# Moving the attention-times-values matmuls of layer 2's rounds to the end of the round

## The chip, the cores and the metric

The kernel runs on one core of a Trainium2 chip. The metric is the device time of one execution in microseconds (us); of several runs the median is given. The engines named below are PE (matrix multiplication, with its weight loads as PEld), DVE (vector), ACT (scalar, activation functions), POOL (a third elementwise engine) and SP (which issues the DMAs here). Each engine runs its instructions strictly in its own order and waits for others by semaphores, so an instruction that waits holds up everything queued behind it.

## The reference

The program computes a transformer of four layers on a batch of B = 4 sequences of S = 512 tokens with D = 128 channels. The change touches layer 2's second attention, a mixture of experts over the value and output projections, with H = 16 heads of P = 64 and E = 8 experts:

```python
def _moe_attn(x, Wq, Wk, Wv, Wo, Wsel_v, Wsel_o):
    q = _rope(jnp.einsum('bsd,hdp->bhsp', x, Wq))
    k = _rope(jnp.einsum('bsd,hdp->bhsp', x, Wk))
    gv = _gate(x, Wsel_v)
    v = jnp.einsum('bsd,bhse,hedp->bhsp', x, gv, Wv)
    att = jax.nn.softmax(jnp.einsum('bhsp,bhtp->bhst', q, k) / np.sqrt(P), axis=-1)
    o = jnp.einsum('bhst,bhtp->bhsp', att, v)
    go = _gate(x, Wsel_o)
    return jnp.einsum('bhsp,bhse,hepd->bsd', o, go, Wo)
```

`_gate` gives each token, for each head, a weight for each of the eight experts (zero for all but two). `_rope` turns the first 32 channels of q and k by the token's position. Everything here is fp32.

## The kernel before, in words

**Rounds.** Layer 2's attention is done in 32 passes, each one sequence and one pair of heads. `l2_ffn` (L1719 on) turns them into 32 rounds and a short 33rd. Round t holds the attention of pass t (`attend`), the output projection of pass t-1 (`finish`), and the projections of pass t+1 (`project`).

`attend(t)` is the round's main list. `score(0, 1)` and `score(2, 3)` (L1811) make for two of the four blocks of 128 queries, and for both heads, a 128 x 512 block of scores (the matmuls `mm<-roped`), and `exps` (L1905) takes each block's maxima on DVE (L1911, written `at_m`) and its exponentials on ACT (L1913, `at_e`), whose sums are kept aside. `turn(i)` (L1820) transposes block i with eight small matmuls (L1825), and ACT copies the result into `eT` (L1826). `invert` (L1828) takes the reciprocals of the sums, transposes them on DVE and sends them to DRAM (`inverted`, L1834). `spread_sums` (L1838) asks for the first part of the output gates `c` (`spread(0)`, the DMAs of L1807) and then brings the reciprocals back over all partitions as `d` (L1843). `values` (L1845) asks for the second part of `c`, multiplies the transposed exponentials by the values in 8 matmuls (L1850) and lets DVE multiply the result by `d` in place (`mm<-mm,d`, the multiplication by d).

`finish(t)` has nine steps `expert(0)` to `expert(8)`: expert e multiplies that result by the gate of expert e on DVE (`og<-mm,c`), and the matmul of expert e-1 (L1878) adds into one PSUM bank. The last step adds the bank into `y`. `project(t)` has ten steps: `rope` (two matmuls, two ACT operations `qk`, two DVE operations `roped`, four DMAs `rot`), eight `value` steps (a matmul `mm<-w_l_ffn_qkv,xT` or the like, and a multiplication by the input gates on DVE, `gvx<-mm,gv`; POOL adds up the experts) and `rope_rest`, two DVE operations.

**The order within a round.** The nineteen steps of `finish` and `project` are merged evenly into one list, the fill:

    rope e0 v0 e1 v1 e2 v2 e3 v3 e4 rope_rest e5 v4 e6 v5 e7 v6 e8 v7

`emit` (L1921) places the fill between the main steps by weights. After each main step it issues fill steps until the share of the fill that is issued equals the share of the weights that is passed:

```python
passed += w
until = len(fill) * passed // total
```

Three rounds are different: in round 16 the fill is not merged (first all of `finish`, then a weight load, then all of `project`), in round 31 it is `finish` alone, and the short 33rd is nothing but `finish`.

**The side chains.** Beside the rounds other work is issued in small steps, by `weave`: a step of the chain for every 3.3 steps of the rounds in rounds 0 to 14 (layer 2's other attentions and gates for sequences 2 and 3), for every 4.5 in rounds 15 to 24 and for every 2.6 in the rest (the dense layers of the finished sequences, layer 3's projections). `dense` is `l2_dense` (L1934). Their usual pieces are statistics of a normalisation on DVE (L470 to L490, ending in `nmr` or `nr_b`), four ACT operations that apply them (L492, `xn` or `d_z`), transposes on PE (L516, L1944) and their copy on ACT (L517), and additions such as `x<-x,...`.

**What sets the order on the engines.** The code is written for a tile framework with a list scheduler: the order in which the steps are issued gives each instruction its priority, and the scheduler then sets each engine's order by that priority and its own estimate of when operands are ready. So a change in the order of the steps moves instructions on every engine, also those of the side chains. PSUM has eight banks, seven of them (`mm`) shared in turn by scores, projections, transposes, the value result and the bank of `finish`; the eighth (`s`) belongs to the side chains. The buffers of `c` are four, those of `eT` two, of `og` three.

Of the kernel before, what the change touches and what calls it, by code (L numbers as in the profile page):

```python
# [291 lines left out]
class Net:  # L292
# [1428 lines left out]
    def l2_ffn(self, pool, gv, y, away, passes, feed, wants, late):  # L1721
# [70 lines left out]
        def attend(t):  # L1792


            b, hp = passes[t]
            m = made[t]
            den = sums[t % 2]
            eT = [pool.tile([P, TB, S], F32, tag=f"eT{hl}", name="eT") for hl in range(2)]
            es = {}

            def spread(part):

                c = m["c", part] = pool.tile([P, 2, S], F32, tag="c", name="c", bufs=4)
                for hl in range(2):
                    at = (2 * hp + hl) * E + 2 * part
                    src = away[b, at : at + 2].rearrange("e s -> (e s)")
                    nc.sync.dma_start(  # L1807
                        c[64 * hl : 64 * hl + 64].rearrange("p e s -> p (e s)"), src.partition_broadcast(64)
                    )

            m["spread"] = spread  # L1811

            def score(*at):
                for i in at:
                    ss = [self.mm() for _ in range(2)]
                    for hl in range(2):
                        r = slice(64 * hl, 64 * hl + 64)
                        self.dot(ss[hl], (m["q"][r, i * P : i * P + P], m["k"][r, :]))
                    es[i] = [self.exps(ss[hl], den[:, TB * hl + i : TB * hl + i + 1], pool, 6) for hl in range(2)]

            def turn(i):
                for hl in range(2):
                    p = self.mm((P, TB, P))
                    for j in range(TB):
                        nc.tensor.transpose(p[:, j, :], es[i][hl][:, j * P : j * P + P], self.ident)  # L1825
                    nc.scalar.copy(eT[hl][:, :, i * P : i * P + P], p)  # L1826

            def invert():  # L1828

                nc.vector.reciprocal(den[:, : 2 * TB], den[:, : 2 * TB])  # L1830
                turned = pool.tile([P, 32], F32, tag="turned", name="turned")
                nc.vector.transpose(turned, den)
                for k in range(4):
                    nc.sync.dma_start(  # L1834
                        inverted[t % 2][:, :, k, :].rearrange("h j r -> (h j) r"), turned[32 * k : 32 * k + 2 * TB, :]
                    )

            def spread_sums():  # L1838
                spread(0)
                m["d"] = pool.tile([P, S], F32, tag="d", name="d")  # L1840
                for hl in range(2):
                    src = inverted[t % 2][hl].rearrange("j k r -> (j k r)")
                    nc.sync.dma_start(m["d"][64 * hl : 64 * hl + 64, :], src.partition_broadcast(64))  # L1843

            def values():  # L1845
                spread(1)
                po = self.mm()
                for j in range(TB):
                    for hl in range(2):
                        nc.tensor.matmul(  # L1850
                            po[64 * hl : 64 * hl + 64, :], lhsT=m["v"][:, j, hl, :], rhs=eT[hl][:, j, :],
                            start=j == 0, stop=j == TB - 1,
                        )
                self.tt(po, po, m.pop("d"), ALU.mult)
                m["o"] = po

            return [
                (lambda: score(0, 1), 4), (lambda: turn(0), 1), (lambda: score(2, 3), 1), (lambda: turn(1), 2),
                (invert, 0), (lambda: turn(2), 2), (lambda: turn(3), 2), (spread_sums, 1), (values, 4),
            ]  # L1860

        def finish(t):
# [26 lines left out]
        def rounds(first, last):  # L1889
            if first == 0:  # L1890
                for step in project(0):
                    step()
                    yield
            for t in range(first, last):
                if t in wants:
                    self.want(wants[t])
                done, new = finish(t - 1), project(min(t + 1, n))
                if t in late:
                    fill = done + [lambda: self.want(late[t])] + new
                else:  # L1900
                    fill = self.merged(done, new)
                yield from self.emit(attend(t) if t < n else [(lambda: None, 1)], fill)
# [606 lines left out]
```

## Time and profile before

| what | us |
|---|---|
| median of 5 runs | 2229.02 |
| lowest and highest run | 2227.91, 2236.06 |
| the profiled execution | 2238.19 |
| its span, first to last instruction | 2236.5 |
| the rounds of layer 2 in it | 925 to 1910 |
| a round, first scores to the next first scores: shortest and longest of the 31 that begin and end in scores | 23.27 (round 0), 37.68 (round 25) |
| a round with no side chain work (15, 24, 30) | 26.96 |

The profiled execution is one run, 9.2 us above the median; differences within it are read from it, and absolute times are compared by medians. In the profile a row of the timeline gives the start, the duration (of a group of like instructions, then with their number behind x), the engine, the source line, the operation with output and input names, and in brackets the idle time that the engine had before it and the instruction that ended the wait. An fp32 matmul shows as two passes, so that "x2" is one matmul over 512 columns; the next group starts while the last pass is still draining, so the pitch from start to start is what PE needs (0.43 a pass), and a group's duration is a little longer.

### The profile page before, as it was taken

The numbers are of one execution on the slowest core, as the hardware profiler recorded it, in microseconds if no ns is written. First come the engines' busy times: TensorE is split into PE (matmuls) and PEld (weight loads), VectorE is DVE, ScalarE is ACT, GpSimd is POOL, SyncE is SP. The second block draws the span as 40 slices with busy tenths as digits, with TensorE's granted clock in tenths as the row PEclk, the third lists the DMA queues.
The fourth block names the chain that finished last, engine by engine and source line by source line (L and its number), as shares of the span: only waits on it lengthen the run. The fifth ranks groups of instructions, "written<-read, shape, count | busy, mean of one in ns | idle before, by whom it ended". The sixth has DMA issues, their size and how long they took to land.

```text
span 2236.5 us, 28168 instructions
## 1 busy us (share of the span) xinstructions
PE 2106.9 (94%) x8982; PEld 1116.6 (50%) x8988; DVE 1604.0 (72%) x4045; ACT 1003.1 (45%) x2040; POOL 568.7 (25%) x705
## 2 busy tenths in 40 slices
PE   6999899999999999899999999999999999699887
PEld 3556556645544554444444444444444444466543
DVE  7676566477675768787977788777866787588735
ACT  4555544543433554344444443434433454156532
POOL 1000000000000000433332334333333354135733
PEclk8898899999999999999999999999999999899978
DMA  6321144254445343334343345445444445321122
GB/s 169 94 72 45 27 122 113 68 127 108 112 103 141 76 122 87 84 87 110 103 120 97 102 120 123 122 108 136 119 132 123 103 124 133 70 96 34 31 73 78
DMA packets 92115, 224.37 MB, mean 100 GB/s; under 512 B 22226, under 2 KB 41106, under 8 KB 91710
## 3 DMA queue, kind: packets, MB, share of 16 engines
q1 hardware_dynamic: 88398, 218.63, 37.0%
q0 software_dynamic: 3568, 3.93, 0.7%
q8 instruction: 71, 1.16, 0.2%
q14 instruction: 78, 0.64, 0.1%
HBM read 193.43 MB, written 23.53 MB: 97 GB/s over the span
## 4 chain that ended last, share of the span: by engine, by line
PE 73%; DVE 17%; ACT 4%; issue 3%; POOL 1%; DMA 1%; another core or an unknown queue 1%; SPq 0%; DVEq 0%; ACTq 0%; POOLq 0%
PE mm L426 19%; PE f L426 13%; PE s L426 8%; PE mm L1878 8%; PE acc L1037 6%; PE mm L1850 5%; PE mm L1825 4%; DVE h L437 2%; PE mm L1205 1%; PE mm L1160 1%; PE mm L1227 1%; DVE m L1167 1%; DVE at_m L1911 1%; DVE x L437 1%; PE acc L2274 1%
## 5 line engine op out<-in xcount | busy, mean ns | idle before, releaser
L1786 POOL TENSOR_TENSOR gvx<-gvx 128x512 f32<-128x512 f32 (+1 forms) x256 | 263.4, 1029 | 537.3 <-DVE gvx L437 459.4
L426 PE MATMUL f<-xT,w_l_ffn 128*128 128x512 f32 (+1 forms) x700 | 338.3, 605 | 1.2 <-ACT h L1029 0.7
L1913 ACT ACTIVATE at_e<-mm,at_m 128x512 f32<-128x512 f32 x256 | 172.9, 685 | 263.6 <-DVE at_m L1911 258.3
L426 PE MATMUL mm<-w_l_ffn_qkv,xT 128*128 128x512 f32 x512 | 265.3, 604 | 4.1 <-ACT at_e L1913 2.0
L1878 PE MATMUL mm<-og,w_l_ffn_o 128*128 128x512 f32 x512 | 263.3, 600 | 3.2 <-DVE og L437 1.9
L437 DVE TENSOR_TENSOR h<-h,f 128x512 f32<-128x512 f32 (+1 forms) x192 | 131.4, 686 | 152.5 <-PE f L426 109.4
L1029 ACT ACTIVATE h<-f 128x512 f32<-128x512 f32 x189 | 112.4, 596 | 246.9 <-PE f L426 209.2
L1037 PE MATMUL acc<-h,w_l_ffn 128*128 128x512 f32 x378 | 198.6, 610 | 3.6 <-DVE h L437 2.9
L426 PEld LDWEIGHTS f<-xT,w_l_ffn 128*128 128x128 f32 (+1 forms) x700 | 126.7, 191 | 133.1 <-issue 112.8
L437 DVE TENSOR_TENSOR gvx<-mm,gv 128x512 f32<-128x512 f32 x256 | 174.3, 684 | 25.7 <-PE mm L426 21.5
L437 DVE TENSOR_TENSOR og<-mm,c 128x512 f32<-128x512 f32 x256 | 173.8, 683 | 22.1 <-PE mm L1878 20.3
L1911 DVE TENSOR_REDUCE at_m<-mm 128x1 f32<-128x512 f32 x256 | 161.5, 683 | 13.0 <-PE mm L426 12.4
L1826 ACT COPY eT<-mm 128x512 f32<-128x512 f32 x256 | 137.3, 595 | 70.1 <-PE mm L1825 69.7
L1825 PEld LDWEIGHTS mm<-ident,at_e 128*128 128x128 f32 x1024 | 119.5, 141 | 66.9 <-issue 46.1
L1878 PEld LDWEIGHTS mm<-og,w_l_ffn_o 128*128 128x128 f32 x512 | 91.1, 190 | 114.9 <-issue 87.6
L1825 PE MATMUL mm<-ident,at_e 128*128 128x128 f32 x1024 | 134.8, 274 | 3.6 <-ACT at_e L1913 3.6
L426 PEld LDWEIGHTS mm<-w_l_ffn_qkv,xT 128*128 128x128 f32 x512 | 87.2, 191 | 92.8 <-issue 54.7
L426 PE MATMUL mm<-roped 64*128 64x512 f32 x512 | 131.2, 623 | 1.6 <-DVE roped L437 1.3
L1167 DVE TENSOR_REDUCE m<-mm 128x1 f32<-128x512 f32 (+3 forms) x176 | 105.5, 637 | 35.5 <-PE mm L1163 34.6
L1850 PE MATMUL mm<-eT,v 128*64 128x512 f32 x512 | 120.8, 606 | 2.1 <-ACT eT L1826 2.1
L1037 PEld LDWEIGHTS acc<-h,w_l_ffn 128*128 128x128 f32 x378 | 72.1, 195 | 89.0 <-issue 62.7
L437 DVE TENSOR_TENSOR h<-h,c 128x512 f32<-128x512 f32 x160 | 110.6, 697 | 3.9 <-DMA c<-l_ffn_w 1.1
(496 smaller groups left out, 3575.8 us busy)
## 6 DMA issues: line engine op xcount, KB each, us to landing
c<-gates SPq DMA_DIRECT2D x256, 256.0 KB
c<-l_ffn_w SPq DMA_DIRECT2D x96, 384.0 KB
w_l_ffn_qkv<-in_l_ffn_qkv SPq DMA_DIRECT2D x24, 640.0 KB
w_l_ffn<-in_l_ffn SPq DMA_DIRECT2D x26, 576.0 KB
w_l_ffn_o<-in_l_ffn_o SPq DMA_DIRECT2D x24, 512.0 KB
rot<-qk SPq DMA_DIRECT2D x128, 64.0 KB
d<-inverted SPq DMA_DIRECT2D x64, 128.0 KB
k_parts<-k SPq DMA_DIRECT2D x12, 384.0 KB
```

Of the source, the lines that this page charges most:

```text
L426: self.nc.tensor.matmul(out, lhsT=lhsT, rhs=rhs, start=i == 0, stop=i == len(pairs) - 1)
L437: self.nc.vector.tensor_tensor(out, a, b, op)
L1029: nc.scalar.activation(h, pg, AF.Silu)
L1037: nc.tensor.matmul(acc["t"], lhsT=W["d" + u], rhs=h, start=i == 0, stop=i == n - 1)
L1167: nc.vector.tensor_reduce(m[:, i, h0 : h0 + per], ps, AX.X, ALU.max, negate=True)
L1786: nc.gpsimd.tensor_tensor(x[:, :, :m], x[:, :, :m], x[:, :, m : 2 * m], ALU.add)
L1825: nc.tensor.transpose(p[:, j, :], es[i][hl][:, j * P : j * P + P], self.ident)
L1826: nc.scalar.copy(eT[hl][:, :, i * P : i * P + P], p)
L1850: nc.tensor.matmul(po[64 * hl : 64 * hl + 64, :], lhsT=m["v"][:, j, hl, :], rhs=eT[hl][:, j, :], start=j == 0, stop=j == TB - 1,)
L1878: nc.tensor.matmul(acc, lhsT=W["o"][:, (e - 1) * D : e * D], rhs=hs.pop(e - 1), start=e == 1, stop=e == E)
L1911: nc.vector.tensor_reduce(m, s, AX.X, ALU.max, negate=True)
L1913: nc.scalar.activation(e[:, :n], s, AF.Exp, bias=m, accum_out=den)
```

## The change

The weights of the last three main steps are changed. `turn(3)` weighs 3 in place of 2, `spread_sums` 4 in place of 1, and `values` 0 in place of 4. The sum of the weights stays 17.

```diff
-                (invert, 0), (lambda: turn(2), 2), (lambda: turn(3), 2), (spread_sums, 1), (values, 4),
+                (invert, 0), (lambda: turn(2), 2), (lambda: turn(3), 3), (spread_sums, 4), (values, 0),
```

With the fill of 19 the order of steps at a round's end becomes, where it was `turn(3), e5, v4, spread_sums, e6, values, v5, e7, v6, e8, v7` and then the next round's `score(0, 1)`: `turn(3), e5, v4, e6, spread_sums, v5, e7, v6, e8, v7, values` and then `score(0, 1)`. In round 31, whose fill is the nine steps of `finish` alone, e6, e7 and e8 stood behind the values and stand ahead of them, and the first steps of `finish(31)` follow the values directly. Nothing is added to or taken from the work.

## The prediction

> **What bounds the kernel now.** I read four views in this order: the page's first lines, the busy time of each engine over the stretch of layer 2's rounds, the waits of PE and DVE in that stretch, and then the timeline of one undisturbed round and of the few rounds with a stall.
>
> The page's head and, below it, the stretch from 925 to 1910 us, which holds all 32 rounds (columns: span of the window, its length, busy time and instruction count of PE, PEld, DVE, ACT, POOL, granted clock, DMA share, GB/s):
>
> ```profile
> span 2236.5 us, 28168 instructions
> PE 2106.9 (94%) x8982; PEld 1116.6 (50%) x8988; DVE 1604.0 (72%) x4045; ACT 1003.1 (45%) x2040; POOL 568.7 (25%) x705
> ...
> 925.00:1910.00 985.00, 962.51 (x3616) 455.33 (x3616) 763.96 (x1479) 428.36 (x990) 363.76 (x436) 0.99 0.44 115
> ```
>
> In the rounds PE is busy 962.5 of 985 us (97.7%), at a clock of 0.99. What PE idles is 22.5 us. The change does not take a single matmul away, so it can win only idle pieces, half-rate pieces and the small cost of changing from one kind of matmul to another.
>
> The undisturbed round 15 on PE (start, duration, line, operation; a trailing bracket would be idle time and its releaser):
>
> ```profile
> 1379.64 0.59 PE L1878 MATMUL mm<-og,w_l_ffn_o 128*128 128x512 f32 x1
> 1380.16 3.65 PE L1850 MATMUL mm<-eT,v 128*64 128x512 f32 x16
> 1383.75 1.12 PE L426 MATMUL mm<-w_l_ffn_qkv,xT 128*128 128x512 f32 x2
> 1384.71 1.02 PE L1878 MATMUL mm<-og,w_l_ffn_o 128*128 128x512 f32 x2
> 1385.57 1.02 PE L426 MATMUL mm<-w_l_ffn_qkv,xT 128*128 128x512 f32 x2
> 1386.43 1.02 PE L1878 MATMUL mm<-og,w_l_ffn_o 128*128 128x512 f32 x2
> 1387.29 1.02 PE L426 MATMUL mm<-w_l_ffn_qkv,xT 128*128 128x512 f32 x2
> 1388.24 1.99 PE L426 MATMUL mm<-roped 64*128 64x512 f32 x8
> ```
>
> No bracket, so no idle. The values (L1850) take 3.65, then come five fill steps, value projections and expert matmuls of 0.86 each, then the next scores at 1388.24. DVE there:
>
> ```profile
> 1383.92 0.70 DVE L437 TENSOR_TENSOR mm<-mm,d 128x512 f32<-128x512 f32 x1 [3.75 <-PE mm L1850]
> ...
> 1389.40 2.49 DVE L1911 TENSOR_REDUCE at_m<-mm 128x1 f32<-128x512 f32 x4
> ```
>
> DVE is idle for 3.75 us while the values run, and the maxima start 1.16 us after the scores. Last, the places where PE stalls, in rounds 9, 18 and 29:
>
> ```profile
> 1211.64 0.71 PE L516 MATMUL s<-ident,xn 128*128 128x128 f32 x2 [1.70 <-ACT xn L492]
> ...
> 1494.35 1.32 PE L1825 MATMUL mm<-ident,at_e 128*128 128x128 f32 x8 [2.77 <-ACT at_e L1913]
> ...
> 1846.87 5.74 PE L1850 MATMUL mm<-eT,v 128*64 128x512 f32 x16 [2.10 <-ACT eT L1826]
> ```
>
> **The change, part by part.** The weights are 17 in sum before and after, so a round keeps its 19 fill steps. With 19 x 12/17 = 13 steps before the sums are spread and 14 before the values, the values stood behind step 14; now turn(3) brings step 14, spread_sums all the rest to 19, and the values come last. Five fill steps (three value projections, two expert matmuls: 5 x 0.86 = 4.3 us of PE) move ahead of the values, and the scores follow the values directly. The instruction order confirms it for PE and also shows the side chains' matmuls moving relative to the round.
>
> *Switches.* A first group behind another kind of matmul reads 1.12 against 1.02 (rows 1383.75 and 1385.57), about 0.09 a switch. Before: into values, out, into scores, out, four; after: into values, values to scores, out, three. One less in 32 rounds: -2.9. Lower end -2.9, upper end 0, if values to scores costs twice; I take -2.9, since both rows show one price whatever the pair. The Trainium skill ("TensorEngine Tiling (Array Packing)", Key Properties) says that changing the tiling mode drains TensorE; no run here shows what values to scores directly costs, and by that rule it is one drain too.
>
> *Split values.* In rounds 25 to 28 side-chain matmuls cut the values into pieces (at 1712.49, 1715.41, 1717.47 and 1719.54 in round 25: 3 cuts, 6 switches, 0.6 us). In the new order they are whole in these: 3 rounds x 0.6 = -1.8; ends 0 and -1.8.
>
> *spread(1) and spread_sums.* Two c DMAs and two d DMAs issue later on SP. SP issues c and d in 1.1 us each and then blocks up to 7.49 us on c buffers, behind d. d gains 3 to 4 fill steps between its issue and its use, so the four waits of DVE for d (8.3 us in all) shrink. They lie beside PE work now: 0. Cover: these five steps of PE work; gone, d's 3.6 us would show.
>
> *turn(3)'s copies.* The values gain 4.3 us over ACT's copies of eT. Only round 29 shows a wait there: 2.10 idle and then 5.74 instead of 3.65, at a granted clock of 0.66 in 1847 to 1852, so 4.2 in sum. But DVE is held there as well: og, which the second expert matmul ahead of the values needs, stands behind a 1.96 us multiplication that ends at 1848.2. PE reaches that expert matmul at about 1845.5 and waits until 1848.8, 3.3 us. Between -4.2 and +2 I take -1.0.
>
> *Round 9.* The xn transposes wait 1.70 behind ACT, which has exps and qk first, and then passes run at a clock of 0.64 for 4 us (1.4 lost): 3.1. In the new order ACT's xn stands ahead of the exps, as it does in round 2 now, where PE idles 0.34 + 0.58. So -2.2; ends -3.1 and 0.
>
> The Trainium skill ("TensorE: Matmul & The Clock Gate", Why this matters for your kernels) warns of idle gaps above about 3 us only. The rows differ: 1.70 and 2.10 idle are followed by 0.64 and 0.66, and 2.77 at 1494 by 1.00. By the rule the 1.4 of round 9 is no consequence of the stall and would stay, and the sum below would be -3.1.
>
> *Round 18.* PE waits 2.77 for at_e, since DVE stands at an x<-x that waits for POOL ahead of two maxima. In the new order x<-x stands behind the first four maxima, six operations sooner. Half of it is won, more or less: -1.5; ends -2.8 and 0. Round 2: 0.9 idle, DVE freer: -0.5; ends -0.9 and 0.
>
> *DVE behind the values.* This is the added wait. The multiplication by d (0.70) waits for the last values matmul; queued behind it are one og and then the maxima. Counted from the scores' start it runs from 0.17 to 0.87 and og to 1.5, first maximum at 1.52 instead of 1.16, and another og among the four: the fourth ends 1.0 later. ACT's fourth exp is then done 5.5 after the scores; PE needs its PSUM bank for the first transposes' second half at 5.88, less 0.14 of signalling. So 0.24 us is spare, and 22 undisturbed rounds lose nothing. In ten rounds (1, 5, 6, 8, 12, 16, 18, 21, 26, 27) the multiplication starts 0.39 to 3.84 after the values' end, against 0.20 to 0.27 in the others, by the timeline of DVE. There the same work lay ahead of the maxima before, so most of it is not new: I take 0.15 each, +1.5. Ends: 0, and +6 if each loses 0.6 (an og).
>
> *Round 26.* PE's xn transposes now stand ahead of the values, 1.7 us earlier in its order, while nmr on DVE is no earlier: +2.3; ends 0 and +2.5. *The end.* The last round has no scores behind it: the experts that ran behind the values stand ahead, and the first new expert matmul waits for the multiplication by d and og: 0.70 + 0.60 + 0.3 of signalling, +1.6; ends +1.3 and +1.8.
>
> Sum: -2.9 - 1.8 + 0 - 1.0 - 2.2 - 1.5 - 0.5 + 1.5 + 2.3 + 1.6 = -4.5. It applies to the profiled execution of 2238.19 (its span is 2236.5, 1.7 us lies around it), which becomes 2233.7; that execution is 9.2 above the median of 2229.02, and I carry the difference over: **2224.5**.
>
> **The rivals.** *No change to speak of* (within 0.2%, 4.5 us, about what a measurement of this kernel can tell from no change): PE is 97.7% busy, undisturbed rounds have no stall to win, and the side-chain stalls just move on to the next instruction; only switches remain less the tail, -2.9 + 1.6, about 2228. For it: each stall is some engine's late side chain. Against: rounds 9 and 18 change their order in ACT and DVE.
>
> *Slower: the maxima are late.* One mechanism: the multiplication by d and an og directly ahead of the maxima. If DVE comes to the multiplication more than 0.24 us later than in round 15, each further microsecond is one of PE idle. For it: the ten late rounds. Against: DVE is idle 3.75 under the values in quiet rounds. If the 31 rounds with scores behind them are 0.74 late, 0.5 x 31 = +15.5, with the other terms of the sum (-6.0) 2238.5. It decides once the loss passes 10.5 us in sum, 0.34 a round.
>
> *Larger gain.* The stalls vanish whole: -2.9 - 1.8 - 4.2 - 3.1 - 2.8 - 0.9 + 1.6 = -14.1, 2215. For it: most have DVE or ACT a few places too late. Against: rounds 26 and 29.
>
> **How the numbers follow.** My forecast, a gain of 2 to 8 (2221 to 2227, its own range): 0.36. Larger gain: 0.20. No change to speak of: 0.10. Slower by the maxima: 0.34. Faster by over 0.2% means below 2224.6, slower above 2233.5. The forecast's centre lies at the first bound: 0.20 of it counts as faster, 0.16 as the same; the larger gain is all faster, no change all the same, the late maxima all slower: 0.40, 0.26, 0.34. The low end, 2211, takes the larger gain, a tail that costs nothing (-1.6) and 2 us of idle pieces not listed, and leaves out 0.05; the high end, 2240, takes the late maxima at 0.8 a round and leaves out 0.12.
>
> **What would show it.** In the profile after: three switch groups a round instead of four; values whole; DVE's idle before the multiplication by d near 3.7 in quiet rounds, first maxima at +1.5; no idle at round 15's transposes; the 1.70 of round 9 gone; an idle of about 1.6 ahead of the last experts. The forecast is wrong if PE shows idle for at_e in many rounds (slower), or if quiet rounds of 26.96 change by over 0.2.

## The result and the profile after

The changed kernel takes 2237.74 us (median of 37 runs) against 2229.02 (63 runs of the kernel before). The ratio is 1.0039, with a 95% interval of 1.0028 to 1.0051: slower by 8.7 us, between 6.2 and 11.4. The forecast was a gain of 4.5.

The page's head of the changed kernel:

```profile
span 2231.5 us, 28205 instructions
PE 2092.7 (94%) x8982; PEld 1117.1 (50%) x8988; DVE 1620.5 (73%) x4045; ACT 1003.1 (45%) x2040; POOL 576.3 (26%) x705
```

The reader must not compare the two spans. This profiled execution is 5 us shorter than the profiled one of the kernel before, although the kernel is slower: the first scores of round 0 come at 918.71 us in place of 925.84, and over all profiles of this study, which do the same work ahead of the rounds (but for five POOL additions in the two kernels without them), they come anywhere from 910.6 to 925.8. So the rounds are compared by themselves, from the first scores of round 0 to the first matmul behind the last round (L1981). Busy time of the engines in that stretch (the columns are those of the windows above), before:

```profile
925.84:1910.64 984.80, 962.51 (x3617) 455.34 (x3617) 763.75 (x1478) 428.36 (x990) 362.93 (x436) 0.99 0.44 115
```

and after:

```profile
918.71:1910.22 991.51, 958.05 (x3617) 460.07 (x3617) 779.84 (x1478) 428.60 (x990) 371.01 (x436) 0.99 0.42 114
```

The stretch is 6.7 us longer, inside the interval of the medians' difference. PE is busy a little less and idles more. DVE does the same 1478 instructions in 16.1 us more, which nothing in the forecast allowed for.

The lengths of the rounds, each worked out as the difference of two starts of first scores in the timeline, show that the loss is not spread. Where the order of a stretch of rounds is the same in two kernels, the lengths mostly agree within 0.02 us, so that small differences can be read:

| round | before | after | difference |
|---|---|---|---|
| 0 | 23.27 | 24.39 | +1.1 |
| 6 | 28.40 | 34.64 | +6.2 |
| 9 | 35.18 | 34.08 | -1.1 |
| 13 | 29.36 | 31.79 | +2.4 |
| 15 and 24, undisturbed | 26.96, 26.97 | 26.89, 26.89 | -0.07, -0.08 |
| 16 | 28.99 | 30.87 | +1.9 |
| 18 | 31.01 | 28.33 | -2.7 |
| 22 | 33.89 | 35.58 | +1.7 |
| 25 | 37.68 | 35.79 | -1.9 |
| 26 | 33.79 | 39.51 | +5.7 |
| 28 | 29.88 | 28.51 | -1.4 |
| 29 | 32.07 | 29.47 | -2.6 |
| 31, to the first matmul behind the rounds | 26.64 | 28.67 | +2.0 |
| the other 18 | | | -4.6 |

The rounds that lose, lose 22.0 us in all, and those that gain, gain 15.3. Round 0 is left out of what follows: it took from 23.1 to 24.4 in the five kernels of this study whose first rounds have the same order and work, so its 1.1 can't be read as an effect.

The waits of PE in the rounds after (what it waited for, total, times, longest):

```profile
PE mm L426 <- ACT at_e L1913: 15.0, 9, 3.8
PE s L516 <- ACT xn L492: 4.3, 1, 4.3
PE mm L1878 <- DVE og L437: 4.1, 5, 1.6
```

The first was 2.0 us in 6 waits before. Value projections wait for a PSUM bank that the exponentials of the scores have not left yet. The four longest of these waits are in rounds 6 (3.80), 13 (3.35), 22 (2.97) and 9 (2.78). The undisturbed round does not have this wait. PE at the end of round 15 after:

```profile
1409.06 1.02 PE L426 MATMUL mm<-w_l_ffn_qkv,xT 128*128 128x512 f32 x2
1410.01 3.65 PE L1850 MATMUL mm<-eT,v 128*64 128x512 f32 x16
1413.59 1.99 PE L426 MATMUL mm<-roped 64*128 64x512 f32 x8
```

and DVE there:

```profile
1413.76 0.70 DVE L437 TENSOR_TENSOR mm<-mm,d 128x512 f32<-128x512 f32 x1 [2.96 <-PE mm L1850]
1414.50 0.69 DVE L437 TENSOR_TENSOR og<-mm,c 128x512 f32<-128x512 f32 x1
1415.11 1.88 DVE L1911 TENSOR_REDUCE at_m<-mm 128x1 f32<-128x512 f32 x3
```

The values stand directly ahead of the scores, DVE waits for them idle, and the first maximum starts 1.52 us after the scores, as worked out; no matmul ahead of the second scores waits for it, and the round as a whole is 0.07 shorter. Now the end of round 5, DVE first:

```profile
1097.01 1.48 DVE L437 TENSOR_TENSOR hi<-go 128x256 f32<-128x256 f32 x1
1098.41 1.21 DVE L437 TENSOR_TENSOR k_work<-k_work,k_n 128x512 f32<-128x512 f32 x1
...
1102.54 1.49 DVE L437 TENSOR_TENSOR lo<-go 128x256 f32<-128x256 f32 x1
1103.95 1.21 DVE L437 TENSOR_TENSOR gv<-gv,k_work 128x512 f32<-128x512 f32 x1
...
1106.28 0.69 DVE L437 TENSOR_TENSOR mm<-mm,d 128x512 f32<-128x512 f32 x1
...
1107.61 2.47 DVE L1911 TENSOR_REDUCE at_m<-mm 128x1 f32<-128x512 f32 x4
```

then PE:

```profile
1099.21 3.65 PE L1850 MATMUL mm<-eT,v 128*64 128x512 f32 x16
1102.79 1.99 PE L426 MATMUL mm<-roped 64*128 64x512 f32 x8
1104.71 1.98 PE L426 MATMUL mm<-xT,w_l_ffn_qkv 128*128 128x512 f32 x4
1110.50 2.07 PE L426 MATMUL mm<-w_l_ffn_qkv,xT 128*128 128x512 f32 x2 [3.80 <-ACT at_e L1913]
1112.36 1.91 PE L1878 MATMUL mm<-og,w_l_ffn_o 128*128 128x512 f32 x2
```

The values end at 1102.7 (by their pitch; the group's last pass drains until 1102.86), but DVE is still in the side chain (layer 2's gates, `hi`, `lo`, `k_work`) and comes to the multiplication by d only at 1106.28, with no idle time ahead of it. The maxima of round 6 start 4.82 us after its scores, PE waits 3.80 (0.15 before), and then runs its passes at half rate, a matmul of 0.86 in 1.7 to 1.9; the granted clock is 0.50 from 1110.4 to 1115.8. The added wait (3.65) and the half rate in the first three groups behind it (about 2.0, worked out below) make 5.7 of the round's 6.2.

Why is DVE so late? Four of its operations took 1.21 to 1.49. In the kernel before the same four took 0.41, 0.68, 0.41 and 0.68:

```profile
1103.26 0.68 DVE L437 TENSOR_TENSOR k_work<-k_work,k_n 128x512 f32<-128x512 f32 x1
1103.86 0.41 DVE L437 TENSOR_TENSOR hi<-go 128x256 f32<-128x256 f32 x1
...
1104.80 0.41 DVE L437 TENSOR_TENSOR lo<-go 128x256 f32<-128x256 f32 x1
...
1106.34 0.68 DVE L437 TENSOR_TENSOR gv<-gv,k_work 128x512 f32<-128x512 f32 x1
```

POOL after, at that time:

```profile
1096.84 2.24 POOL L1786 TENSOR_TENSOR gvx<-gvx 128x512 f32<-128x512 f32 x2 [0.26 <-DVE gvx L437]
1099.15 0.78 POOL L1787 TENSOR_TENSOR v<-gvx 128x128 f32<-128x128 f32 x1
1102.10 2.51 POOL L1786 TENSOR_TENSOR gvx<-gvx 128x512 f32<-128x512 f32 x2 [2.17 <-DVE gvx L437]
```

Each long operation of DVE lies where POOL adds up the values of the eight experts. The kernel before on POOL:

```profile
1101.47 0.76 POOL L1688 COPY k_work<-k_work 128x128 f32<-128x128 f32 x2
1107.70 2.07 POOL L1786 TENSOR_TENSOR gvx<-gvx 128x512 f32<-128x512 f32 x2 [5.47 <-DVE gvx L437]
```

So there POOL finished its work at 1102.2 and did not begin again until 1107.7; the value steps came behind the attention's values. The change moves three value steps ahead of them, and POOL's additions with them, onto the very stretch in which DVE has the side chain's last work to do.

### The profile page after: what moved, and what is told of

Its sections match the earlier page's. It is cut to its first block, busy times and chain, and to the rows that moved or that the text cites. A ratio compares the mean times of both kernels' runs of the same rounds, so it can differ in the third digit from the quotient of the medians.

```text
span 2231.5 us, 28205 instructions
## 1 busy us (share of the span) xinstructions
PE 2092.7 (94%) x8982; PEld 1117.1 (50%) x8988; DVE 1620.5 (73%) x4045; ACT 1003.1 (45%) x2040; POOL 576.3 (26%) x705
## 4 chain that ended last, share of the span: by engine, by line
PE 71%; DVE 19%; ACT 3%; issue 3%; POOL 1%; DMA 1%; another core or an unknown queue 1%; SPq 0%; DVEq 0%; ACTq 0%; POOLq 0%
PE mm L426 20%; PE f L426 12%; PE mm L1878 8%; PE s L426 8%; PE acc L1037 6%; PE mm L1825 4%; PE mm L1850 4%; DVE h L437 2%; PE mm L1160 2%; DVE at_m L1911 2%; PE mm L1227 1%; PE mm L1205 1%; DVE x L437 1%; DVE gvx L437 1%; PE acc L2274 1%
## 5 line engine op out<-in xcount | busy, mean ns | idle before, releaser
L426 PE MATMUL mm<-w_l_ffn_qkv,xT 128*128 128x512 f32 x512 | 264.3, 602 | 16.1 <-ACT at_e L1913 15.0
L492 ACT ACTIVATE xn<-x,nmr,rstd 128x128 f32<-128x128 f32 x188 | 78.5, 483 | 93.9 <-DVE nmr L490 92.5
```

Source lines behind the costliest of these rows:

```text
L426: self.nc.tensor.matmul(out, lhsT=lhsT, rhs=rhs, start=i == 0, stop=i == len(pairs) - 1)
```

## The experiments

In all of them `t` is the round; "old weights" are those of the kernel before. They ran on two chips, on which the kernel before took 2208.0 (the first four) and 2208.5 (the last three), so ratios are compared, and the stretches of the rounds. Each stretch is that of one profiled execution. In a kernel with a line added above them the source lines are one higher, in the two without POOL's additions two lower.

### Old weights where DVE is late

```diff
+            a, z, w = (2, 1, 4) if t in (5, 12, 21) else (3, 4, 0)
             return [
...
-                (invert, 0), (lambda: turn(2), 2), (lambda: turn(3), 3), (spread_sums, 4), (values, 0),
+                (invert, 0), (lambda: turn(2), 2), (lambda: turn(3), a), (spread_sums, z), (values, w),
```

> The changed kernel, but rounds 5, 12 and 21 keep the old weights (2, 1, 4): the rounds at whose end DVE, behind side-chain work, reaches the multiplication by d 3.6 to 4.1 us late in the profile after. Theory A (the loss is DVE's lateness in a few rounds, paid at the maxima of the next): rounds 6, 13 and 22 were 6.2, 2.4 and 1.7 us longer than before and give that back, about 10 us less than the changed kernel, so 2227 or 0.999 of the kernel before. Theory B (the loss is spread: the multiplication and og directly ahead of the maxima cost each round a little): three of 31 rounds give back under 1 us, 2237.

Measured: ratio to the kernel before 1.0000 (0.9979 to 1.0020), where the change alone had 1.0039. The stretch is 985.84, 5.7 us less than after. Rounds 6, 13 and 22 fall from 34.64, 31.79 and 35.58 to 29.68, 30.04 and 33.70, 8.6 us together. Against that, round 9 is 1.5 and round 26 is 1.7 longer than after. Theory A holds for these rounds, and B, which allowed under 1 us, does not: the three give back 8.6 of the 10.4 that they had lost. They are not the whole, since the losing rounds lost 22.0 in all.

### Old weights in round 26 and in the last

The same edit with `t in (26, 31)`.

> The changed kernel, but rounds 26 and 31 keep the old weights. Theory A': the transposes of xn that stand ahead of the values in round 26 (that round is 5.7 us longer in the profile after) and the last round's wait for the first experts (2.0) are a second, separate loss, and 7.7 us come back: 2230, about 1.0005 of the kernel before. Theory B: under 1 us comes back, 2237.

Measured: 1.0003 (0.9981 to 1.0026); the stretch is 983.78, 7.7 less than after. Round 26 falls from 39.51 to 35.63, the last from 28.67 to 27.01, and two rounds that the edit doesn't touch are shorter too, round 0 by 1.3 and round 6 by 1.0; the others agree. So the two rounds give back 5.5, not the 7.7 that was expected of them; that the stretch fell by just 7.7 is chance. What PE did in round 26 after:

```profile
1754.20 0.86 PE L516 MATMUL s<-ident,xn 128*128 128x128 f32 x2 [4.29 <-ACT xn L492]
1754.85 1.92 PE L426 MATMUL mm<-w_l_ffn_qkv,xT 128*128 128x512 f32 x2
1756.56 0.63 PE L516 MATMUL s<-ident,xn 128*128 128x128 f32 x2
1757.87 1.12 PE L426 MATMUL mm<-xT,w_s 128*128 128x512 f32 x2 [0.68 <-ACT xT L517]
1758.93 3.65 PE L1850 MATMUL mm<-eT,v 128*64 128x512 f32 x16
```

The transposes of xn wait 4.29 for ACT's xn, which waits for statistics on DVE, and xT another 0.68. Before, the wait was 1.21: the values (3.65) and two fill steps stood ahead of the transposes.

### All of these places at once

The same edit with `t in (5, 12, 16, 21, 26, 31)`.

> Old weights in rounds 5, 12, 16, 21, 26 and 31, the new ones in the others. Theory A and A' together: 10.3 + 7.7 + 1.9 (round 16) = 20 us less than the changed kernel, 2218, and so faster than the kernel before by 0.5%, since the gains of the other rounds (15 us in the profile) stay. Theory B: 2235, no faster than before. Third possibility: moved steps shift the side chains and new late places appear, between 2222 and 2230.

Measured: 2199.87 against 2208.0, ratio 0.9967 (0.9946 to 0.9988); the stretch is 976.47, 15.0 less than after and 8.3 less than before. So it beats both. Theory B is out: nothing was done for the other 26 rounds, and what they pay for the new order is less than what they gain by it. The size is short of the 20 us: rounds 6, 13 and 16 (29.66, 30.05, 30.27) came back only in part, and round 9 is 1.5 longer.

### Three fill steps behind the values

```diff
-(invert, 0), (lambda: turn(2), 2), (lambda: turn(3), 3), (spread_sums, 4), (values, 0),
+(invert, 0), (lambda: turn(2), 2), (lambda: turn(3), 3), (spread_sums, 2), (values, 2),
```

> Weights 3, 2 and 2 in all rounds: the values stand behind two more fill steps than before, and three fill steps (v6, e8, v7: 2.6 us of PE) remain between them and the next scores. Theory A: a lateness of DVE of 3.6 to 4.1 us is covered to 2.6 + 0.24, 0.8 to 1.3 us remain in each of the three rounds, so the loss there falls from 10.3 to about 3, with the tail still at about 1.6: 2229 to 2231. Theory B: no round has the multiplication directly ahead of the maxima any more, so all of the spread loss goes: 2228. It tells A from B only by the lengths of rounds 6, 13 and 22, which keep 0.8 to 1.3 each by A.

Measured: 1.0002 (0.9981 to 1.0023); the stretch is 984.41. Rounds 6, 13 and 22 are 29.73, 30.63 and 34.91, which is 1.3, 1.3 and 1.0 above the kernel before, as theory A has it. The undisturbed rounds are 26.96 and 26.97 again: with fill between values and scores their 0.07 is gone. This place of the values is worth no more than the old one.

### POOL's additions left out

Twice the same edit, in the kernel before and in the changed one. Both leave out the addition of experts 2 to 7, so they compute something else and serve for their times alone.

```diff
                 if hl:
                     x = gx[j]
-                    for m in (4, 2):
-                        nc.gpsimd.tensor_tensor(x[:, :, :m], x[:, :, :m], x[:, :, m : 2 * m], ALU.add)
                     nc.gpsimd.tensor_tensor(v[:, j], x[:, :, 0], x[:, :, 1], ALU.add)
```

> The kernel before without the two POOL additions that add the eight experts' values down to two (L1786); the values are then made from experts 0 and 1 alone. A reference for the next run: POOL has 263 us less, PE and DVE have the same instructions. Theory C (DVE's side-chain operations are held while POOL works on the same SBUF): DVE's busy time falls by some 15 us in the rounds, and the kernel gains little, 0 to 5 us in the rounds' stretch of 984.8, since the lateness was covered. Rival (DVE's lateness is only the number of its operations): DVE's busy time and the stretch stay within 1 us, since neither PE nor DVE loses an instruction.

> The changed kernel with the same two POOL additions left out (values from experts 0 and 1 alone). Theory C: in the changed order POOL adds v4 to v7 just while DVE does the side chain's work ahead of the multiplication by d, and four such operations of round 5 took 1.21 to 1.49 us where they took 0.41 to 0.68 before. Without the additions they take the short times again, the multiplication at the end of rounds 5, 8, 12 and 21 is under 1.5 us late in place of 3.6 to 4.1, rounds 6, 13 and 22 fall from 34.6, 31.8 and 35.6 to below 30.5, 30 and 34, and the loss against the run without additions of the kernel before falls from 6.7 us in the stretch to about 1 or below nothing. Rival: the lateness is the number of operations; rounds 6, 13 and 22 stay above 33, 31 and 35, and the loss against the other run stays at 5 to 8 us.

Measured: 0.9927 (0.9904 to 0.9951) for the order before and 0.9898 (0.9861 to 0.9935) for the changed order, both against the unaltered kernel before. The intervals overlap; the rounds settle it. The order before:

```profile
921.64:1891.11 969.47, 955.76 (x3618) 453.37 (x3617) 749.65 (x1478) 428.61 (x990) 109.28 (x184) 1.00 0.44 117
```

The changed order:

```profile
914.17:1876.18 962.01, 946.55 (x3618) 455.99 (x3617) 751.79 (x1478) 428.12 (x990) 116.42 (x184) 1.00 0.43 117
```

Without the additions the change makes the rounds 7.5 us shorter; with them, 6.7 longer. DVE's busy time falls by 14.1 in the order before and by 28.1 in the changed one, with the same instructions: POOL held DVE twice as long in the changed order. Rounds 6, 13 and 22 are 27.95, 28.46 and 32.72, at most 0.1 longer than those of the order before without the additions (28.07, 28.37, 33.80). The order of DVE's operations at the end of round 5 is the same as after. The four of them take the short times but for one, and the multiplication comes 0.31 after the values' end in place of 3.58 (the four had cost 3.2 more than their short times):

```profile
1087.82 0.42 DVE L437 TENSOR_TENSOR hi<-go 128x256 f32<-128x256 f32 x1
1088.16 0.69 DVE L437 TENSOR_TENSOR k_work<-k_work,k_n 128x512 f32<-128x512 f32 x1
...
1091.78 0.68 DVE L437 TENSOR_TENSOR lo<-go 128x256 f32<-128x256 f32 x1
1092.38 0.68 DVE L437 TENSOR_TENSOR gv<-gv,k_work 128x512 f32<-128x512 f32 x1
...
1093.92 0.69 DVE L437 TENSOR_TENSOR mm<-mm,d 128x512 f32<-128x512 f32 x1
```

Two things went otherwise than expected. At the end of round 21 the multiplication is still 2.26 late (under 1.5 was expected): there DVE also stands 3.5 us at an addition that waits for POOL's part of the dense layer. And the order before gained 15.3 us in its rounds, where 0 to 5 had been expected: the holding cost the kernel before as well, in rounds 2, 9, 26, 29 and others. In round 26 3.1 of the 5.7 us stay without the additions (34.91 against 31.79, with a wait of 2.93 for xn), so that loss is for the larger part one of order, not of POOL.

### A second mixture

The edit with `t in (5, 6, 12, 13, 15, 16, 21, 26, 31)`.

> Old weights in rounds 5, 6, 12, 13, 15, 16, 21, 26 and 31: the earlier mixture with 6, 13 and 15 added, since rounds 6, 13 and 16 were still 1.3, 0.7 and 1.3 us longer than before in it. If a round's length depends only on its own order and on the end of the round ahead, rounds 6, 13 and 16 return to 28.4, 29.4 and 29.0, and the stretch falls from 976.5 to 973.2, 0.995 of the kernel before in all. Rival: the side chains shift with each change of order, so the gain is anything from -3 to +3.

Measured: 0.9965 (0.9944 to 0.9987), a stretch of 973.21. The sum is the expected one, but not by the expected parts. Round 16 returned to 28.99: its own old weights had taken 0.6 off its loss of 1.9 in the first mixture, those of round 15 now take the other 1.3; rounds 6 and 13 did not (29.00 and 30.23 where 28.4 and 29.4 were expected). 1.5 of the 3.3 us are round 9, whose order was not touched. Whether this mixture is faster than the first is not settled by these runs.

## Why the prediction was wrong

**The step that failed** is "DVE behind the values", and in it the sentence that in the ten late rounds the same work lay ahead of the maxima before, "so most of it is not new: I take 0.15 each, +1.5. Ends: 0, and +6". Rounds 6, 13 and 22 alone lost 10.4, above the upper end. Two things were wrong in it. First, the lateness at the end of rounds 5 and 12 is new: counted like the prediction's 0.39 to 3.84 it was 0.39 and 1.35 in the kernel before and is 3.58 and 3.66 after. The side chain's work was much the same, but its durations were taken from the rows of the old order, and at the end of round 5 POOL is idle there. The run without POOL's additions shows this: with them gone, the lateness is 0.31 and 1.34, and the step costs those rounds nothing. Second, the late rounds lost the 4.3 us of PE's fill steps that had stood between values and scores and had let DVE catch up, and the prediction's own rule, 0.24 us to spare, was set aside for them. At the end of round 21 the lateness is hardly new (3.84 before, 4.08 after) and was among the prediction's own figures; there the fill behind the values had hidden part of it. With three fill steps put back (2.6 us), rounds 6, 13 and 22 lose 1.0 to 1.3 each. A half rate behind the stall came on top: in round 6 the first three groups behind it start 1.86, 1.71 and 1.71 us apart where 0.97, 0.86 and 1.42 had been (the last with a wait of 0.39 and a switch), about 2 of the 6.2.

The mechanism was named as the rival on the slower side, with its threshold of 0.24 us, and given 0.34. Its price assumed the same loss of 0.5 in all rounds; the trace shows it in a few, where it is several times larger. That its 2238.5 lies next to the measured 2237.7 is chance.

**Round 26** was put at +2.3 with +2.5 as the end; it was +5.7, for a wait of 4.29 + 0.68 in place of 1.21 and one matmul of 1.7 in place of 0.86 behind it. The step took PE 1.7 sooner and "nmr on DVE ... no earlier". The second half is wrong: nmr's operation ended 28.35 us after the round's first scores before and 30.62 after, 2.3 later; 1.65 of this are three small operations of its chain that take 1.25, 0.57 and 0.31 in place of 0.16 each, beside POOL's additions. **The end** cost 2.0 (1.6 was taken): the wait itself is 1.63.

**Terms that came near by luck.** *Switches* were put at 0.09 each. Rounds 3, 4, 10, 14, 19 and 23 gained 0.19 to 0.20 each, and in the kernel with three fill steps behind the values, which has as many switches as the kernel before, they have their old lengths again. A switch lengthens the pitch of the group ahead of it too: in the rows of round 15 before, the last fill step ahead of the scores takes 0.95 (from 1387.29 to 1388.24) in place of 0.86, as the first one behind the values does (0.96). The prediction counted one side. From values directly to scores a switch cost about the same: in round 15 after, 0.10 on the last pass of the values and 0.10 on the first of the scores. The undisturbed rounds gained only 0.07 to 0.08, because they did lose something: the second scores, before and after, in round 15:

```profile
1395.52 1.99 PE L426 MATMUL mm<-roped 64*128 64x512 f32 x8
...
1393.98 2.11 PE L426 MATMUL mm<-roped 64*128 64x512 f32 x8
```

So "lose nothing" is wrong by 0.12 a round there, and 0.07 agrees with 0.09 by luck. *Split values*: the prediction read pieces in rounds 25 to 28, but in 26, 27 and 28 the values were whole in the kernel before, as the row of 3.65 at 1749.77 shows for round 26. Only round 25's were cut. It gained 1.9, which meets the 1.8 taken for three rounds by chance; round 28 gained 1.4, where a wait of 1.27 for at_e ahead of an expert matmul is gone.

```profile
1749.77 3.65 PE L1850 MATMUL mm<-eT,v 128*64 128x512 f32 x16
```

**What was right.** The timing of the quiet rounds: the fourth exponential ends 5.47 us after the scores of round 15 (5.5 was worked out), and no transposes wait for it. Round 18 gained 2.7 (1.5), round 29 2.6 less 0.6 in round 30 (1.0). Round 9 gained 1.1 (2.2): the 1.70 for xn is gone, but 2.78 for at_e came in its place. Round 2 gained nothing (0.5). The step on spread_sums was right that d would not be waited for where it had been; no wait of DVE for d is left among its larger ones.

**Not seen:** round 16. There, where all experts come first, the second one waits 1.00 for an og behind the maxima; old weights in rounds 15 and 16 together took its loss away, those of round 16 alone 0.6 of the 1.9.

## What to carry to other kernels

A step's durations on DVE were true only for the place they were measured at; when steps that feed POOL are moved, look at what DVE does at their new place. A chain in which each engine waits for the one before (values, multiplication, maxima, exponentials, banks) needs as much other PE work inside it as its slowest round is late, and a mean over the rounds says nothing on that: give each round the order that suits it, as the mixture did (0.9967). And compare the stretch that a change touches, not two profiled spans.

## What the runs showed of the hardware

POOL's additions can stretch DVE operations whose operands all lie in SBUF, even the smallest: in round 26 after, a 128 x 4 operation took 1.25 us in place of 0.16. Not all of them: the statistics `st` (L484) and `mv` (L485), with one input, began 30 times within such an addition in the changed kernel's rounds and took at most 0.30, as elsewhere. And `og` and `gvx`, which read PSUM, kept 0.63 to 0.69 throughout. The Trainium skill says of this ("SBUF — State Buffer", Terms) that DVE and GpSimd arbitrate for a shared port pair, exclusively and for a whole instruction, so that the loser blocks; "GPSIMD Engine Reference", Specifications, limits it to DVE instructions in a two-port mode or with two SBUF inputs. The rows agree with both.

The half rate behind a stall is not a matter of its length alone. In round 9 the changed kernel and the one with old weights in rounds 5, 12 and 21 both wait 2.78 for at_e. After:

```profile
1209.63 1.13 PE L426 MATMUL mm<-w_l_ffn_qkv,xT 128*128 128x512 f32 x2 [2.78 <-ACT at_e L1913]
1210.59 1.02 PE L1878 MATMUL mm<-og,w_l_ffn_o 128*128 128x512 f32 x2
```

With old weights in those three:

```profile
1201.03 1.12 PE L426 MATMUL mm<-w_l_ffn_qkv,xT 128*128 128x512 f32 x2 [2.78 <-ACT at_e L1914]
1201.99 1.77 PE L1879 MATMUL mm<-og,w_l_ffn_o 128*128 128x512 f32 x2
```

The granted clock is 1.00 in the 4 us behind the first and 0.65 in the 5 us behind the second, which makes 1.5 us of round 9. So the length of the stall does not decide it; what does, these runs don't show. A difference of 1.5 us in one round can come from this alone, with the work and the stall unchanged. The Trainium skill ("TensorE: Matmul & The Clock Gate", Why this matters for your kernels) has a limit of about 3 us for such gaps; the second pair of rows shows half rate below it, so here the limit does not hold.
